# Splitting the state of a graph network's recurrence into two exact float32r parts for the aggregation by a 0/1 adjacency

## The chip, the cores and the metric

The kernel runs on one core of a Trainium2 chip. TensorE (PE in the profile) multiplies matrices and writes its results to PSUM; VectorE (DVE), ScalarE (ACT) and GpSimd (POOL) do elementwise work; SyncE (SP) issues the transfers. Each engine works through its own list of instructions in order, and waits at an instruction whose inputs are not there yet. The metric is the device time of one execution in microseconds (us), and the figure for a kernel is the median of its runs.

## The reference

The input is a batch of 128 graphs of 128 nodes with 256 features, and a 0/1 adjacency matrix for each graph. Four layers follow, each with a residual and a layer normalization:

- layer 0: attention with four edge types (scores by x scaled with a0 to a3, a softmax, a weighted sum of nodes),
- layer 1: a mean over neighbours of x W_msg, added to x W_upd, with a relu,
- layer 2: a gated recurrence of three steps,
- layer 3: attention by two vectors, a softmax, and an elu.

The change is in layer 2:

```
A = (adj != 0).astype(x.dtype)
h = x
for i in range(3):
    m = einsum('bnd,de->bne', h, weight[i])
    aggr = einsum('bst,bsd->btd', A, m)
    h = gru_cell(aggr, h, w_ih, w_hh, b_ih, b_hh)
```

All values are float32. The entries of A are 0 or 1.

## The kernel before

The 128 graphs are taken in 32 groups of four (G = 4, NG = 32), so that a tile of one half of the features (KC = 2 halves, c = 0 and 1, of 128) for a group is 128 x 512. A group passes through three generators: `head` (layers 0 and 1, ending with x2, the input of the recurrence), `gru` (layer 2, NL = 3 steps) and `tail` (layer 3 and the output).

The aggregation is moved ahead of the weight: since A^T (h W_i) w_ih^T = (A^T h) (W_i w_ih^T), the product W_i w_ih^T is made once at the start (c_gi, L158), and each step multiplies only the state h by the adjacency. `aggregate(c)` (L386 to L393) does that for one half of the features: four products of 128 x 128 by 128 x 128, one for each graph, with the state (nodes as rows, `hn[c]`) as the stationary operand and the mask a_ne as the moving one. ScalarE copies the result out of PSUM to agT (L393), which then multiplies c_gi in the gates (L401).

The state is kept with the features as rows (hT), as the gates want it. For the aggregation it must have the nodes as rows. In step 0, `hn` is a view of x2 itself (L367). In steps 1 and 2, `h_tokens` (L376) transposes hT by TensorE (L373) and copies the result out of PSUM: on ScalarE for c = 0, on VectorE for c = 1 (L378). For c = 0 it is called before the last gate of the step before (L467), for c = 1 after the first products of the step (L443), with two 128x512 products of L401 (L445, L446) between its transposes and `aggregate(1)`.

The gates follow: reset (L412), candidate (L418) and update (L426), each with ScalarE for the activation and VectorE for the arithmetic, and with one subtraction on GpSimd (L423).

While `gru` of group g runs, `head` of group g+1 and `tail` of group g-1 run beside it. `run` (L569) interleaves the three: each generator yields the TensorE time that it has just put out and the gap until it wants to go on, and `run` lets a side line go on when a clock made of these sums has passed its due time; a third value False says that the next piece has no TensorE work. This gives the order of TensorE's products. On the other engines the order in the built program is a list of its own, and pieces of different generators stand among each other there: on VectorE, the masks of the next group (L277) stand among the message step of this one (L343 to L351).

A layernorm (L183) goes over three engines: statistics on VectorE (L191, L192), a power on GpSimd (L196), then L198 and L201 on VectorE and L207 on ScalarE.

Tiles come from pools with a number of buffers for each tag: `hn` has 3, the layernorm's outputs have 2 (`xa`, x1 of layer 1), 4 (`xb`, shared by x2 and the output y) and 2 (`xa3`, x3 of layer 3). [...]

Of the kernel before, what the change touches and what calls it, by code (L numbers as in the profile page):

```python
# [7 lines left out]

F32 = mybir.dt.float32
U8 = mybir.dt.uint8  # L10
I32 = mybir.dt.int32
AF = mybir.ActivationFunctionType
# [5 lines left out]
def kernel(  # L18
# [30 lines left out]
    nc = tc.nc  # L49
    B, N, D = x.shape  # L50
    P = 128
    assert N == P and D == 2 * P
    G = 4
    NG = B // G
    T = G * N
    KC = D // P
# [49 lines left out]
    work = ctx.enter_context(tc.tile_pool(name="work", bufs=2))  # L106
# [76 lines left out]
    def layernorm(res, tag, bufs, out):  # L183


        mv = work.tile([P, G, 2], F32, tag="mv", name="mv", bufs=4)
        rstd = work.tile([P, G], F32, tag="rstd", name="rstd", bufs=4)
        nmr = work.tile([P, G], F32, tag="nmr", name="nmr", bufs=4)
        for b in range(G):
            st = work.tile([P, 6], F32, tag="st", name="st", bufs=8)  # L190
            nc.vector.bn_stats(st, res[:, b, :])  # L191
            nc.vector.bn_aggr(mv[:, b, :], st)  # L192
            if b == 1:
                yield 0.0, 1.5, False
        nc.vector.tensor_scalar_add(rstd, mv[:, :, 1], EPS)  # L195
        nc.gpsimd.tensor_tensor(rstd, rstd, neg_half, OP.pow)  # L196
        yield 0.0, 2.5, False
        nc.vector.scalar_tensor_tensor(nmr, mv[:, :, 0], -1.0, rstd, op0=OP.mult, op1=OP.mult)  # L198
        xn = work.tile([P, G, D], F32, tag=tag, name=tag, bufs=bufs)
        for b in range(0, G, 2):  # L200
            nc.vector.tensor_scalar(  # L201
                xn[:, b, :], res[:, b, :], mv[:, b, 0:1], rstd[:, b : b + 1],
                op0=OP.subtract, op1=OP.mult,
            )
        yield 0.0, 0.5, False
        for b in range(1, G, 2):
            nc.scalar.activation(  # L207
                xn[:, b, :], res[:, b, :], AF.Identity, bias=nmr[:, b : b + 1], scale=rstd[:, b : b + 1]
            )
        out.append(xn)  # L210
# [38 lines left out]
    def leaky(out, in_, bias):  # L249
        nc.scalar.activation(out, in_, AF.Prelu, bias=bias, scale=1.0, alpha=SLOPE)  # L250

    FLAT = "p b n -> p (b n)"


# [4 lines left out]
    def head(g, s):  # L259
# [8 lines left out]
        nc.gpsimd.memset(alpha, NEG0 / SLOPE)  # L268
        mk = work.tile([P, 4, G, N], U8, tag="mk", name="mk")
        s.m_gt = work.tile([P, G, N], U8, tag="m_gt", name="m_gt", bufs=3)  # L270
        s.a_ne = work.tile([P, G, N], F32, tag="a_ne", name="a_ne")


        xT = features_first(xg, "xT", 4)
# [1 line left out]
        for k in range(4):  # L276
            nc.vector.tensor_scalar(mk[:, k], a_f, float(k + 1), None, op0=OP.is_equal)  # L277
            yield 0.0, 1.0
            ps = bank()
            xs = []  # L280
            for c in range(KC):
                t = work.tile([P, T], F32, tag="xs", name="xs", bufs=4)
# [16 lines left out]
        got = []  # L299
# [6 lines left out]
        res = work.tile([P, G, D], F32, tag="res", name="res", bufs=3)  # L306
# [10 lines left out]
                )  # L317
        yield 1.75, 2.0, False
        got = []
        yield from layernorm(res, "xa", 2, got)  # L320
        x1 = got[0]
        yield 0.0, 2.0

# [30 lines left out]
            if b % 2:  # L354
                yield 0.9, 2.5, b == 1
        got = []
        yield from layernorm(res, "xb", 4, got)
        s.x2 = got[0]
        yield 0.0, 2.0
        s.hT = features_first(s.x2, "hT", 6)  # L360
        yield 0.9, 1.5

# [1 line left out]

    def gru(s):
        hT = s.hT
        hn = [s.x2[:, :, c * P : (c + 1) * P] for c in range(KC)]  # L367

        def tokens_first(c, h):

            ps = bank()
            for b in range(G):
                nc.tensor.transpose(ps[:, b * N : (b + 1) * N], h[:, b * N : (b + 1) * N], ident)  # L373
            return ps.rearrange("p (b d) -> p b d", b=G)

        def h_tokens(c, h):  # L376
            t = work.tile([P, G, P], F32, tag="hn", name="hn", bufs=3)
            (nc.scalar.copy if c == 0 else nc.vector.tensor_copy)(t, tokens_first(c, h))  # L378
            return t

        for i in range(NL):
            agT = [None] * KC
            new = [None] * KC
            gates = {}

            def aggregate(c):  # L386
                ps = bank()
                for b in range(G):
                    nc.tensor.matmul(  # L389
                        ps[:, b * N : (b + 1) * N], hn[c][:, b, :], s.a_ne[:, b, :], start=True, stop=True  # L390
                    )
                agT[c] = work.tile([P, T], F32, tag="agT", name="agT", bufs=3)
                nc.scalar.copy(agT[c], ps)  # L393

            def terms(q, of_h=(), of_m=(), start=False, stop=False):

                if start:
                    gates[q] = bank()
                ops = [(w_hhT[:, c], hT[c]) for c in of_h] + [(c_gi[:, i, c], agT[c]) for c in of_m]
                for n, (w, v) in enumerate(ops):  # L400
                    nc.tensor.matmul(  # L401
                        gates[q], w[:, q * P : (q + 1) * P], v,
                        start=(start and n == 0), stop=(stop and n == len(ops) - 1),
                    )
                return gates.pop(q) if stop else None

            def hidden(c, ps):
                t = work.tile([P, T], F32, tag="q", name="q", bufs=3)
                nc.scalar.activation(t, ps, AF.Identity, bias=bhn[:, c : c + 1], scale=0.5)  # L409
                return t  # L410

            def reset(c, ps, q):  # L412
                t = work.tile([P, T], F32, tag="t_r", name="t_r")
                nc.scalar.activation(t, ps, AF.Tanh, bias=brz[:, c : c + 1], scale=0.5)  # L414
                nc.vector.scalar_tensor_tensor(t, t, 1.0, q, op0=OP.add, op1=OP.mult)  # L415
                return t

            def candidate(c, ps, t):  # L418
                nc.vector.tensor_add(t, t, ps)  # L419
                n = work.tile([P, T], F32, tag="t_n", name="t_n")  # L420
                nc.scalar.activation(n, t, AF.Tanh, bias=bih[:, 2 * KC + c : 2 * KC + c + 1], scale=1.0)  # L421
                d = work.tile([P, T], F32, tag="t_d", name="t_d")
                nc.gpsimd.tensor_sub(d, hT[c], n)  # L423
                return n, d

            def update(c, ps, n, d):  # L426

                z = work.tile([P, T], F32, tag="t_z", name="t_z")
                nc.scalar.activation(z, ps, AF.Tanh, bias=brz[:, KC + c : KC + c + 1], scale=0.5)  # L429
                nc.vector.scalar_tensor_tensor(d, z, 1.0, d, op0=OP.add, op1=OP.mult)  # L430
                new[c] = work.tile([P, T], F32, tag="hT", name="hT", bufs=6)
                nc.vector.scalar_tensor_tensor(new[c], d, 0.5, n, op0=OP.mult, op1=OP.add)

            R, Z, C = 0, KC, 2 * KC
            aggregate(0)
            yield 0.9, 0.0
            terms(C, of_h=[0], start=True)
            terms(R, of_h=[0], start=True)
            yield 1.7, 0.0
            terms(C + 1, of_h=[0], start=True)  # L440
            yield 0.85, 0.0
            if i:
                hn[1] = h_tokens(1, hT[1])  # L443
                yield 0.45, 0.0
            q0 = hidden(0, terms(C, of_h=[1], stop=True))  # L445
            terms(R, of_h=[1])  # L446
            yield 1.7, 0.0
            aggregate(1)
            yield 0.9, 0.0
            q1 = hidden(1, terms(C + 1, of_h=[1], stop=True))  # L450
            yield 0.85, 0.0
            t0 = reset(0, terms(R, of_m=[0, 1], stop=True), q0)
            yield 1.7, 0.0
            n0, d0 = candidate(0, terms(C, of_m=[0, 1], start=True, stop=True), t0)
            yield 1.7, 0.0
            terms(Z, of_h=[0, 1], start=True)
            yield 1.7, 0.0
            update(0, terms(Z, of_m=[0, 1], stop=True), n0, d0)
            yield 1.7, 0.0
            terms(R + 1, of_h=[0, 1], start=True)  # L460
            yield 1.7, 0.0
            t1 = reset(1, terms(R + 1, of_m=[0, 1], stop=True), q1)
            yield 1.7, 0.0
            n1, d1 = candidate(1, terms(C + 1, of_m=[0, 1], start=True, stop=True), t1)
            yield 1.7, 0.0
            if i < NL - 1:
                first = h_tokens(0, new[0])  # L467
                yield 0.45, 0.0
            terms(Z + 1, of_h=[0, 1], start=True)
            yield 1.7, 0.0  # L470
            update(1, terms(Z + 1, of_m=[0, 1], stop=True), n1, d1)
            yield 1.7, 0.0
            if i < NL - 1:
                hn = [first, None]
            hT = new
        s.hT = hT
        s.tokens_first = tokens_first


    def tail(g, s):  # L480
# [4 lines left out]
            nc.vector.tensor_add(res[:, :, cols], s.tokens_first(c, s.hT[c]), s.x2[:, :, cols])  # L485
        yield 0.9, 2.0, False
        got = []
        yield from layernorm(res, "xa3", 2, got)
        x3 = got[0]
        yield 0.0, 2.0  # L490
        xT = features_first(x3, "xT", 4)
# [52 lines left out]
            nc.vector.scalar_tensor_tensor(res[:, half], neg[:, half], -1.0, res[:, half], op0=OP.add, op1=OP.add)  # L544
            yield 0.0, 1.0, False
        got = []
        yield from layernorm(res, "xb", 4, got)
        y = got[0]
        nc.sync.dma_start(out=out[g * G : (g + 1) * G].rearrange("b n d -> n b d"), in_=y)
        yield 0.0, 0.0  # L550
# [79 lines left out]
```

## Time and profile before

| | |
|---|---|
| median of 3 runs | 3250.92 us (3248.24 to 3251.22) |
| profiled execution | 3248.32 us, its span 3246.5 us |
| TensorE busy | 3172.2 us, 98% |
| VectorE, ScalarE, GpSimd busy | 1504.8, 1379.7, 724.7 us (46%, 42%, 22%) |
| granted TensorE clock | 0.993 |
| L401, gate products (two groups of 2304 records) | 1079.8 and 1072.7 us busy |
| L389, aggregation (1024 and 512 records) | 137.5 and 68.4 us busy |
| L373, transposes of the state (768 records) | 110.2 us busy |
| one group in the steady part (1029.65 to 1128.53 us) | 98.9 us |

The span is the time from the first to the last instruction of the profiled execution. A group's line in the profile names the source line, the engine, the operation, the tiles written and read, and the number of records; "mean ns" is the length of one record, which is longer than the distance between two of them, since TensorE's products overlap. The busy time counts overlapping records once. The idle time at the end of a line is that of the engine just before these instructions, with what ended it.

### The profile page before, as it was taken

The numbers are of one execution on the slowest core, as the hardware profiler recorded it, in microseconds if no ns is written. First come the engines' busy times: TensorE is split into PE (matmuls) and PEld (weight loads), VectorE is DVE, ScalarE is ACT, GpSimd is POOL, SyncE is SP. The second block draws the span as 40 slices with busy tenths as digits, with TensorE's granted clock in tenths as the row PEclk, the third lists the DMA queues.
The fourth block names the chain that finished last, engine by engine and source line by source line (L and its number), as shares of the span: only waits on it lengthen the run. The fifth ranks groups of instructions, "written<-read, shape, count | busy, mean of one in ns | idle before, by whom it ended". The sixth has DMA issues, their size and how long they took to land.

```text
span 3246.5 us, 33653 instructions
## 1 busy us (share of the span) xinstructions
PE 3172.2 (98%) x12244; PEld 1854.0 (57%) x12244; DVE 1504.8 (46%) x4019; ACT 1379.7 (42%) x2832; POOL 724.7 (22%) x615
## 2 busy tenths in 40 slices
PE   7999999999999999999999999999999999999996
PEld 5565555565555555555655555555556555555653
DVE  3454444544444544444444445444545344454443
ACT  3344444444444444444444444444444444444443
POOL 2122222222221222221222222222212222222211
PEclk9999999999999999999999999999999999999997
DMA  2000000000000000000000000000000000000000
GB/s 80 10 17 7 17 10 17 17 14 10 10 17 17 17 7 17 10 17 17 14 10 11 16 17 17 8 16 10 17 17 17 7 17 10 14 14 7 1 7 13
DMA packets 56997, 47.65 MB, mean 15 GB/s; under 512 B 4352, under 2 KB 56704, under 8 KB 56832
## 3 DMA queue, kind: packets, MB, share of 16 engines
q1 hardware_dynamic: 56832, 45.50, 4.4%
q8 instruction: 98, 1.61, 0.2%
q14 instruction: 67, 0.55, 0.1%
HBM read 28.72 MB, written 16.78 MB: 14 GB/s over the span
## 4 chain that ended last, share of the span: by engine, by line
PE 90%; DVE 5%; POOL 2%; ACT 1%; issue 1%; DMA 0%; SPq 0%; ACTq 0%; POOLq 0%; DVEq 0%
PE ps L401 56%; PE ps L291 7%; PE ps L332 7%; PE ps L389 5%; PE ps L219 4%; PE ps L497 4%; PE ps L373 2%; PE ps L530 2%; PE ps L341 2%; PE ps L311 2%; DVE mk L277 1%; POOL rstd L196 1%; POOL a_f L266 1%; PE ps L244 1%; DVE res L348 1%
## 5 line engine op out<-in xcount | busy, mean ns | idle before, releaser
L401 PE MATMUL ps<-agT,c_gi 128*128 128x512 f32 x2304 | 1072.7, 595 | 13.5 <-ACT agT L393 13.1
L401 PE MATMUL ps<-hT,w_hhT 128*128 128x512 f32 x2304 | 1079.8, 593 | 0.0
L401 PEld LDWEIGHTS ps<-agT,c_gi 128*128 128x128 f32 x2304 | 423.1, 190 | 512.5 <-issue 447.2
L401 PEld LDWEIGHTS ps<-hT,w_hhT 128*128 128x128 f32 x2304 | 410.6, 190 | 345.5 <-issue 325.0
L430 DVE SCALAR_TENSOR_TENSOR t_d<-t_z,t_d 128x512 f32<-128x512 f32 x192 | 132.4, 689 | 711.5 <-ACT t_z L429 711.5
L423 POOL TENSOR_TENSOR t_d<-hT,t_n 128x512 f32<-128x512 f32 x192 | 247.8, 1290 | 928.8 <-ACT t_n L421 928.8
L291 PEld LDWEIGHTS ps<-xs,xT 128*128 128x128 f32 x2048 | 248.7, 192 | 60.7 <-issue 46.6
L429 ACT ACTIVATE t_z<-ps,brz 128x512 f32<-128x512 f32 x192 | 131.9, 687 | 349.3 <-PE ps L401 349.3
L196 POOL TENSOR_TENSOR rstd<-rstd,neg_half 128x4 f32<-128x4 f32 x128 | 130.3, 1018 | 627.5 <-DVE rstd L195 627.3
L415 DVE SCALAR_TENSOR_TENSOR t_r<-t_r,q 128x512 f32<-128x512 f32 x192 | 132.4, 690 | 294.2 <-ACT t_r L414 294.2
L284 POOL TENSOR_SCALAR xs<-xT,acol 128x512 f32<-128x512 f32 x128 | 201.5, 1578 | 260.1 <-PE ps L291 166.5
L291 PE MATMUL ps<-xs,xT 128*128 128x128 f32 x2048 | 249.3, 275 | 0.0
L332 PE MATMUL ps<-w_um,xT 128*128 128x512 f32 x512 | 240.9, 594 | 0.5 <-ACT xT L220 0.5
L421 ACT ACTIVATE t_n<-t_r,bih 128x512 f32<-128x512 f32 x192 | 138.2, 720 | 212.7 <-DVE t_r L419 212.7
L409 ACT ACTIVATE q<-ps,bhn 128x512 f32<-128x512 f32 x192 | 131.1, 683 | 212.7 <-PE ps L401 212.7
L191 DVE BATCH_NORM_STATS2 st<-res 128x6 f32<-128x256 f32 x512 | 200.5, 408 | 2.1
L414 ACT ACTIVATE t_r<-ps,brz 128x512 f32<-128x512 f32 x192 | 130.8, 681 | 143.5 <-PE ps L401 139.5
L292 DVE COPY_PREDICATED alpha<-mk,ps 128x512 f32<-128x512 uint8 x128 | 93.1, 728 | 189.7 <-PE ps L291 189.7
L389 PEld LDWEIGHTS ps<-a_ne,hn 128*128 128x128 f32 x1024 | 132.7, 192 | 66.0 <-ACT q L409 31.7
L207 ACT ACTIVATE xb<-res,nmr,rstd 128x256 f32<-128x256 f32 x128 | 72.8, 595 | 218.0 <-DVE nmr L198 211.9
L332 PEld LDWEIGHTS ps<-w_um,xT 128*128 128x128 f32 x512 | 95.1, 191 | 108.3 <-issue 99.5
L419 DVE TENSOR_TENSOR t_r<-t_r,ps 128x512 f32<-128x512 f32 x192 | 131.8, 686 | 34.8 <-PE ps L401 28.2
(92 smaller groups left out, 3458.9 us busy)
## 6 DMA issues: line engine op xcount, KB each, us to landing
x_in<-in_x_dram SPq DMA_DIRECT2D x32, 512.0 KB, 3.9
out_dram<-xb SPq DMA_DIRECT2D x32, 512.0 KB, 2.9
adj_in<-in_adj_dram SPq DMA_DIRECT2D x32, 256.0 KB, 2.8
nat<-in_L_gnn_w_ih_dram SPq DMA_DIRECT2D x1, 768.0 KB, 4.9
wnat<-in_L_gnn_weight_dram SPq DMA_DIRECT2D x3, 256.0 KB, 5.2
nat<-in_L_gnn_w_hh_dram SPq DMA_DIRECT2D x1, 768.0 KB, 7.0
w_um<-in_L_gnn_W_upd_dram SPq DMA_DIRECT2D x1, 256.0 KB, 7.3
w_um<-in_L_gnn_W_msg_dram SPq DMA_DIRECT2D x1, 256.0 KB, 7.2
```

Source lines behind the costliest of these rows:

```text
L191: nc.vector.bn_stats(st, res[:, b, :])
L196: nc.gpsimd.tensor_tensor(rstd, rstd, neg_half, OP.pow)
L284: nc.gpsimd.tensor_scalar(t, xT[c], acol[:, k, c : c + 1], None, op0=OP.mult)
L291: nc.tensor.matmul(ps[:, cols], xT[c][:, cols], xs[c][:, cols], start=(c == 0), stop=(c == KC - 1))
L332: nc.tensor.matmul(ps, xT[c][:, b * N : (b + 1) * N], w_um[:, c, :], start=(c == 0), stop=(c == KC - 1))
L389: nc.tensor.matmul(ps[:, b * N : (b + 1) * N], hn[c][:, b, :], s.a_ne[:, b, :], start=True, stop=True)
L401: nc.tensor.matmul(gates[q], w[:, q * P : (q + 1) * P], v, start=(start and n == 0), stop=(stop and n == len(ops) - 1),)
L415: nc.vector.scalar_tensor_tensor(t, t, 1.0, q, op0=OP.add, op1=OP.mult)
L421: nc.scalar.activation(n, t, AF.Tanh, bias=bih[:, 2 * KC + c : 2 * KC + c + 1], scale=1.0)
L423: nc.gpsimd.tensor_sub(d, hT[c], n)
L429: nc.scalar.activation(z, ps, AF.Tanh, bias=brz[:, KC + c : KC + c + 1], scale=0.5)
L430: nc.vector.scalar_tensor_tensor(d, z, 1.0, d, op0=OP.add, op1=OP.mult)
```

## The change

The mask a_ne becomes a float32r tile. A new helper, `halves`, takes a piece of the state v and writes hi, v rounded to float32r, on ScalarE, and then lo = v - hi, also float32r, on an engine that is given. [...] `aggregate` multiplies hi and lo by the mask in turn and lets PSUM add them: eight products with float32r operands in place of four with float32.

In steps 1 and 2, `h_tokens` makes both parts from the transposed state in PSUM, hi on ScalarE and lo on VectorE, for both values of c. In step 0 the parts of x2 are made at the end of `head`, hi on ScalarE and lo on GpSimd, before x2's transposes, with yields of their own. `hi` and `lo` have 4 buffers each in place of the 3 of `hn`; the buffers of `xa`, `xb` and `xa3` go from 2, 4 and 2 to 1, 3 and 1.

```diff
@@ -7,6 +7,9 @@
 from concourse._compat import with_exitstack
 
 F32 = mybir.dt.float32
+
+
+F32R = mybir.dt.float32r
 U8 = mybir.dt.uint8
 I32 = mybir.dt.int32
 AF = mybir.ActivationFunctionType
@@ -249,6 +252,14 @@
     def leaky(out, in_, bias):
         nc.scalar.activation(out, in_, AF.Prelu, bias=bias, scale=1.0, alpha=SLOPE)
 
+    def halves(v, lo_engine):
+
+        hi = work.tile([P, G, P], F32R, tag="hi", name="hi", bufs=4)
+        lo = work.tile([P, G, P], F32R, tag="lo", name="lo", bufs=4)
+        nc.scalar.copy(hi, v)
+        lo_engine.tensor_sub(lo, v, hi.bitcast(F32))
+        return hi, lo
+
     FLAT = "p b n -> p (b n)"
 
 
@@ -268,7 +279,7 @@
         nc.gpsimd.memset(alpha, NEG0 / SLOPE)
         mk = work.tile([P, 4, G, N], U8, tag="mk", name="mk")
         s.m_gt = work.tile([P, G, N], U8, tag="m_gt", name="m_gt", bufs=3)
-        s.a_ne = work.tile([P, G, N], F32, tag="a_ne", name="a_ne")
+        s.a_ne = work.tile([P, G, N], F32R, tag="a_ne", name="a_ne")
 
 
         xT = features_first(xg, "xT", 4)
@@ -317,7 +328,7 @@
                 )
         yield 1.75, 2.0, False
         got = []
-        yield from layernorm(res, "xa", 2, got)
+        yield from layernorm(res, "xa", 1, got)
         x1 = got[0]
         yield 0.0, 2.0
 
@@ -354,9 +365,13 @@
             if b % 2:
                 yield 0.9, 2.5, b == 1
         got = []
-        yield from layernorm(res, "xb", 4, got)
+        yield from layernorm(res, "xb", 3, got)
         s.x2 = got[0]
-        yield 0.0, 2.0
+        yield 0.0, 1.0, False
+        s.hn = []
+        for c in range(KC):
+            s.hn.append(halves(s.x2[:, :, c * P : (c + 1) * P], nc.gpsimd))
+            yield 0.0, 0.5, c == KC - 1
         s.hT = features_first(s.x2, "hT", 6)
         yield 0.9, 1.5
 
@@ -364,7 +379,8 @@
 
     def gru(s):
         hT = s.hT
-        hn = [s.x2[:, :, c * P : (c + 1) * P] for c in range(KC)]
+
+        hn = s.hn
 
         def tokens_first(c, h):
 
@@ -374,9 +390,7 @@
             return ps.rearrange("p (b d) -> p b d", b=G)
 
         def h_tokens(c, h):
-            t = work.tile([P, G, P], F32, tag="hn", name="hn", bufs=3)
-            (nc.scalar.copy if c == 0 else nc.vector.tensor_copy)(t, tokens_first(c, h))
-            return t
+            return halves(tokens_first(c, h), nc.vector)
 
         for i in range(NL):
             agT = [None] * KC
@@ -386,9 +400,11 @@
             def aggregate(c):
                 ps = bank()
                 for b in range(G):
-                    nc.tensor.matmul(
-                        ps[:, b * N : (b + 1) * N], hn[c][:, b, :], s.a_ne[:, b, :], start=True, stop=True
-                    )
+                    for v in hn[c]:
+                        nc.tensor.matmul(
+                            ps[:, b * N : (b + 1) * N], v[:, b, :], s.a_ne[:, b, :],
+                            start=(v is hn[c][0]), stop=(v is hn[c][1]),
+                        )
                 agT[c] = work.tile([P, T], F32, tag="agT", name="agT", bufs=3)
                 nc.scalar.copy(agT[c], ps)
 
@@ -485,7 +501,7 @@
             nc.vector.tensor_add(res[:, :, cols], s.tokens_first(c, s.hT[c]), s.x2[:, :, cols])
         yield 0.9, 2.0, False
         got = []
-        yield from layernorm(res, "xa3", 2, got)
+        yield from layernorm(res, "xa3", 1, got)
         x3 = got[0]
         yield 0.0, 2.0
         xT = features_first(x3, "xT", 4)
@@ -544,7 +560,7 @@
             nc.vector.scalar_tensor_tensor(res[:, half], neg[:, half], -1.0, res[:, half], op0=OP.add, op1=OP.add)
             yield 0.0, 1.0, False
         got = []
-        yield from layernorm(res, "xb", 4, got)
+        yield from layernorm(res, "xb", 3, got)
         y = got[0]
         nc.sync.dma_start(out=out[g * G : (g + 1) * G].rearrange("b n d -> n b d"), in_=y)
         yield 0.0, 0.0
```

## The prediction

> **What bounds the kernel now.** I read the page first (busy shares and the chain that ended last), then the groups by form, then what TensorE waited for, then the timeline of one period. The page:
>
> ```profile
> PE 3172.2 (98%) x12244; PEld 1854.0 (57%) x12244; DVE 1504.8 (46%) x4019; ACT 1379.7 (42%) x2832; POOL 724.7 (22%) x615
> ...
> PE 90%; DVE 5%; POOL 2%; ACT 1%; issue 1%; DMA 0%; SPq 0%; ACTq 0%; POOLq 0%; DVEq 0%
> ```
>
> TensorE has work in 98% of the span and is 90% of the last chain; the other engines have room on average. So the time moves with TensorE's own work and with every new hole in it. The groups that the change touches, and two that serve as prices (the last number before the bar is the count, then busy us and mean ns of one):
>
> ```profile
> L423 POOL TENSOR_TENSOR t_d<-hT,t_n 128x512 f32<-128x512 f32 x192 | 247.8, 1290 | 928.8 <-ACT t_n L421 928.8
> ...
> L389 PE MATMUL ps<-a_ne,hn 128*128 128x128 f32 x1024 | 137.5, 277 | 9.3 <-DVE mv L192 9.3
> ...
> L419 DVE TENSOR_TENSOR t_r<-t_r,ps 128x512 f32<-128x512 f32 x192 | 131.8, 686 | 34.8 <-PE ps L401 28.2
> ...
> L389 PE MATMUL ps<-a_ne,xb 128*128 128x128 f32 x512 | 68.4, 277 | 0.0
> ...
> L378 DVE COPY hn<-ps 128x512 f32<-128x512 f32 x64 | 43.5, 679 | 3.4 <-PE ps L373 3.4
> ...
> L378 ACT COPY hn<-ps 128x512 f32<-128x512 f32 x64 | 37.2, 582 | 2.8 <-PE ps L373 1.0
> ```
>
> L389 is the aggregation: 32 groups x 3 layers x 2 halves x 4 graphs = 768 products, and 1536 records, so each float32 product is two passes. Its busy time is 205.9 us, 6% of the span: that is all the change can touch. What matters more is where TensorE waits inside a period (98.9 us, from one L373 of layer 2 at 1029.65 us to the same one at 1128.53). It waits at two places, once per period:
>
> ```profile
> PE ps L401 <- ACT agT L393: 13.1, 28, 0.5
> PE ps L389 <- DVE mv L192: 9.3, 28, 0.3
> ```
>
> Both belong to the second half (c = 1) of layer 2. The timeline there (start, duration, idle before in brackets), called place B:
>
> ```profile
> 1029.65 0.60 PE L373 MATMUL ps<-ident,hT 128*128 128x128 f32 x4
> ...
> 1031.47 0.68 DVE L378 COPY hn<-ps 128x512 f32<-128x512 f32 x1
> ...
> 1032.30 1.13 PE L389 MATMUL ps<-a_ne,hn 128*128 128x128 f32 x8 [0.33 <-DVE mv L192]
> ...
> 1033.25 1.01 POOL L196 TENSOR_TENSOR rstd<-rstd,neg_half 128x4 f32<-128x4 f32 x1 [2.13 <-DVE rstd L195]
> ...
> 1034.49 0.60 ACT L207 ACTIVATE xb<-res,nmr,rstd 128x256 f32<-128x256 f32 x1 [2.65 <-DVE nmr L198]
> 1034.99 0.56 ACT L393 COPY agT<-ps 128x512 f32<-128x512 f32 x1
> ...
> 1035.61 2.84 PE L401 MATMUL ps<-agT,c_gi 128*128 128x512 f32 x6 [0.47 <-ACT agT L393]
> ```
>
> The transposed state is ready at 1030.25, but the copy starts at 1031.47, behind the next graphs' message step on VectorE; the waiter's label (mv) is a neighbour, the copy is what ends at 1032.15. Then agT stands behind a layernorm line on ScalarE. The same step of layer 1, place A, lies 35 us earlier in a period:
>
> ```profile
> 994.46 0.60 PE L373 MATMUL ps<-ident,hT 128*128 128x128 f32 x4
> ...
> 995.33 0.67 DVE L378 COPY hn<-ps 128x512 f32<-128x512 f32 x1
> ...
> 996.31 0.16 DVE L195 TENSOR_SCALAR rstd<-mv 128x4 f32<-128x4 f32 x1
> 996.55 1.01 POOL L196 TENSOR_TENSOR rstd<-rstd,neg_half 128x4 f32<-128x4 f32 x1 [12.37 <-DVE rstd L195]
> 996.62 1.05 PE L389 MATMUL ps<-a_ne,hn 128*128 128x128 f32 x8
> ```
>
> Between the last transpose and the aggregation TensorE has two products of 0.86 us, so the copy has 1.72 us; here it finishes 0.6 us early.
>
> [...]
>
> **The change, part by part.**
> *TensorE.* Each product of two passes becomes two single-pass products (high, low), so 1536 passes stay 1536. Now eight passes of L389 take 0.89 us (1025.32 to 1026.21), 111 ns each. No row shows a float32r product. The nearest single pass over four-byte data is the transpose: L373, four from 1018.86 to 1019.30, 110 ns each, for 128 columns. [...] upper bound 222 ns (a whole float32 product each). I take 109: [...] Sum: 1536 x (109 - 111) = -3 us. Ends: [...] 1536 x +111 = +170 us.
>
> *Splitting the state, layers 1 and 2.* Before: one copy per half (ACT for c = 0, DVE for c = 1). After: ACT writes hi, then DVE subtracts: 64 more ACT copies at 582 ns (37 us) and 64 more DVE operations at 686 (44 us), against idle shares of 58% and 54%. For c = 0 this hides: after the transposes at 982.77 the aggregation comes at 990.55, 7.8 us for a chain of 0.6 + 0.7; in layer 2 (1018.86 to 1025.32) 6.5 us, and VectorE has idle time before L343 that takes the subtraction up but for 0.1 us. Were that cover gone, 0.7 us each.
>
> For c = 1 it does not hide. Without any queue the chain is 0.60 (transposes) + 0.58 + 0.69 + hand-overs of some 0.1 = 2.0 us against 2.16; all queueing comes on top, and the built order of the changed kernel shows what stands ahead.
>
> Place A: ScalarE has hi behind two of the exp lines (L232); VectorE has lo behind the whole layernorm of the head: all four L191, L516, L227, then L195, L198 (which waits for the power on GpSimd) and both L201. From 992.60, at the spacings of before (L191 0.32, L516 0.60, L227 0.59, with L192 0.08 to 0.1): L516 starts at 994.14 instead of 993.34, the maximum L227 ends at 995.58, L195 at 995.66, the power runs to 996.75, L198, two L201, lo from 997.53 to 998.20. hi is there at 997.0 (two exp at 0.40 from 995.61, then 0.58). The first low product starts at 998.27, seven more passes, and the next product at 999.04 instead of 997.51: 1.53 us late. agT, which costs a gap of 0.28 in the products behind it now (the row of four at 998.37 takes 2.17 instead of 1.88), is then in time. Net 1.25 us.
>
> Place B: VectorE has one mask (L277), one L191 and one L192 more ahead of lo than it had ahead of the copy (0.33 + 0.33 + 0.08), so lo runs 1032.26 to 1032.94 and the aggregation ends 0.5 us later. The layernorm behind it slides too: L195 1033.06, power to 1034.32, L207 at 1034.55 and 1035.05. ScalarE's order is now both L207, hi of the next group's x2 (0.6, itself waiting for the second L207), and only then agT: 1036.2 to 1036.8. TensorE's L401 resumes at 1036.85 instead of 1035.61: 1.24 us. The first half's delay lies inside this.
>
> Sum: 2.5 us per period. 28 periods show both old waits; I count 29 for edges: 72 us.
>
> *x2's own halves, layer 0.* Two ACT copies and two POOL subtractions (1290 ns by L423) a group: on POOL from 1036.3 to 38.9, before L423 needs it at 1041.3; TensorE needs them a good 10 us later. The one uncovered case is the first group, where aggregation follows at once: some 2 us, once.
>
> *Order and buffers.* TensorE's order is unchanged but for the x2 transposes, one pair of products later, with 6.9 us until use: nothing. xa and xa3 at one buffer: x1 lives until L351 and x3 until L540, within one period each: nothing. xb at three: y takes the buffer of the x2 that its tail read first, x2 that of a y sent out almost a period before: nothing; a wait would cost about a power round trip, 1.3 us a period. The mask a_ne in float32r: same count and shape, nothing. DMA is untouched.
>
> Total: -3 + 72 + 2 = +71 us on the profiled 3248.3 (span 3246.5), 3319. The median of the runs stands 2.6 higher, 3250.9, so 3322; I say 3321.
>
> **Rivals.**
> (1) A float32r product of only 128 columns costs as much as a float32 product. For: nothing shows that the single pass is quick at this shape. Against: the transposes. +170 in place of -3, of which place B's sixth (28) hides behind agT's wait: 3321 + 173 - 28 = 3466.
> (2) The one that ends faster: [...] Outside place B 1280 passes gain 111 - p. It decides at p = 111 - 74/1.28 = 53 ns with waits as worked, at p = 111 - 38/1.28 = 81 with waits half as long (36 us, and the 2 of the start). [...]
> (3) The waits do not come, since the layernorm ahead of lo runs earlier than I put it: 3321 - 72 = 3249, no change.
>
> **How the numbers follow.** Forecast 63%, own range 3285 to 3360 (1.2 to 3.8 us a period). (1) 17%. (2) 14%: half of it faster, the rest split between equal and slower. (3) 6%. The range 3225 to 3400 leaves out (1) and the lower end of (2), two in ten. Faster or slower means by more than 0.2%, 6.5 us, about what a measurement of this kernel can tell from no change: faster 0.07, same 0.08, slower 0.85.
>
> **What would show it.** Aggregation passes 109 to 112 ns apart: the even trade; [...] TensorE's waits: the subtraction ahead of the aggregation some 1.3 us, once a period, place A; agT ahead of L401 grown from 0.47 to above 1 us, place B. A period of 101.4 us instead of 98.9. I am wrong if the period is within 0.3 us of the old one, or if waits appear at c = 0 or layer 0.

## The result and the profile after

The changed kernel takes 3358.61 us (median of 4 runs, 3358.08 to 3360.88) against 3250.79 us for the kernel before in the same measurement: a ratio of 1.0335, 95% interval 1.0317 to 1.0353. Its profiled span is 3356.9 us, 110.4 us more than the 3246.5 of before. That hi is the state rounded to float32r, and that hi and lo together give it back exactly, as the title has it, is the intent of the change; no run here measures it.

The page of the changed kernel, busy time and the chain that ended last:

```profile
PE 3196.9 (95%) x12244; PEld 1864.5 (56%) x12244; DVE 1563.8 (47%) x4083; ACT 1457.8 (43%) x2960; POOL 794.2 (24%) x679
...
PE 62%; DVE 22%; ACT 7%; POOL 5%; issue 3%; DMA 0%; ACTq 0%; DVEq 0%; POOLq 0%; SPq 0%
```

TensorE has exactly the 12244 records of before, and its share of the last chain has gone from 90% to 62%, with VectorE from 5% to 22%. TensorE's waits (who waited for whom, us in total, times, longest):

```profile
PE ps L404 <- DVE lo L260: 71.5, 61, 2.3
PE ps L417 <- ACT agT L409: 30.0, 28, 1.1
```

These stand where before had 9.3 and 13.1 us. (L404 is the aggregation, L417 the gate products, L260 the subtraction, L409 the copy to agT.) Place A, the second half of the state in layer 1, on all engines:

```profile
1027.03 1.11 POOL L199 TENSOR_TENSOR rstd<-rstd,neg_half 128x4 f32<-128x4 f32 x1 [11.52 <-DVE rstd L198]
...
1027.69 0.56 ACT L259 CAST hi<-ps 128x512 fp32r<-128x512 f32 x1
...
1028.17 0.16 DVE L201 SCALAR_TENSOR_TENSOR nmr<-mv,rstd 128x4 f32<-128x4 f32 x1 [0.90 <-POOL rstd L199]
1028.25 0.73 DVE L204 TENSOR_SCALAR xa<-res,mv,rstd 128x256 f32<-128x256 f32 x2
...
1028.31 0.33 PE L404 MATMUL ps<-a_ne,hi 128*128 128x128 f32 x1 [0.24 <-ACT hi L259]
...
1028.90 0.68 DVE L260 TENSOR_TENSOR lo<-ps,hi 128x512 fp32r<-128x512 f32 x1
...
1029.63 0.33 PE L404 MATMUL ps<-a_ne,lo 128*128 128x128 f32 x1 [1.00 <-DVE lo L260]
...
1030.47 1.72 PE L417 MATMUL ps<-hT,w_hhT 128*128 128x512 f32 x2
...
1031.98 4.69 PE L417 MATMUL ps<-agT,c_gi 128*128 128x512 f32 x8
...
1133.97 1.07 PE L417 MATMUL ps<-hT,w_hhT 128*128 128x512 f32 x2
...
1134.88 3.60 PE L417 MATMUL ps<-agT,c_gi 128*128 128x512 f32 x8
```

The high part is ready at 1028.25. VectorE, though, is in the layernorm: it waits 0.90 us for GpSimd's power, then writes xa twice, and only then subtracts. TensorE stands still for most of that time: it waits 0.24 us for hi, runs one product, and waits 1.00 us for lo. The last four lines are the next thing that TensorE does, in this period and in the next one. The same ten passes take 6.04 us from 1030.47 to the next product, and 4.34 us one period later. No wait lies in them: the granted clock is 0.59 in the 4 us from 1030.00 (0.50 from 1030.76 to 1034.17) and 1.00 in the 4 us from 1133.00. The stretches of the changed kernel (from:to, length, then busy time of each engine, and the granted TensorE clock ahead of the DMA share):

```profile
1030.00:1034.00 4.00, 4.00 (x11) 2.03 (x11) 0.00 (x0) 1.86 (x4) 0.19 (x1) 0.59 0.00 0
...
1133.00:1137.00 4.00, 3.87 (x14) 2.22 (x15) 0.26 (x2) 2.56 (x7) 0.53 (x1) 1.00 0.00 0
```

Place B, the second half in layer 2:

```profile
1067.77 0.33 PE L404 MATMUL ps<-a_ne,lo 128*128 128x128 f32 x1 [1.31 <-DVE lo L260]
...
1069.32 1.09 ACT L210 ACTIVATE xb<-res,nmr,rstd 128x256 f32<-128x256 f32 x2 [3.06 <-DVE nmr L201]
1070.45 0.62 ACT L259 CAST hi<-xb 128x512 fp32r<-128x512 f32 x1
1070.97 0.58 ACT L409 COPY agT<-ps 128x512 f32<-128x512 f32 x1
...
1071.60 2.84 PE L417 MATMUL ps<-agT,c_gi 128*128 128x512 f32 x6 [1.07 <-ACT agT L409]
```

Here ScalarE has agT behind both of its writes of xb and behind the first copy of x2. Before, agT stood between the two writes of xb, and there was no copy of x2.

TensorE's starts give an account of a steady period, 98.88 us before and 101.80 after, and 103.50 in ten of the 30 periods, with one exception every third. From the transposes of place A to the probabilities' transposes (L244 before, L247 after) it is 7.62 us before and 9.06 after: +1.44. From the transposes of place B to the second product on agT it is 5.96 and 7.53: +1.57. The other steps differ by little, -0.1 in all. The periods of 103.50 have 1.70 more, half of the 3.41 us for which the granted clock is 0.50. Over the 30 periods the sum is 103 us, of which some 86 are waits and some 17 (ten periods) the clock. The other 7 lie at the start and the end.

### The profile page after: what moved, and what is told of

Read it like the earlier page. It is cut to its first block, busy times and chain, and to the rows that moved or that the text cites. A ratio compares the mean times of both kernels' runs of the same rounds, so it can differ in the third digit from the quotient of the medians.

```text
span 3356.9 us, 33791 instructions
## 1 busy us (share of the span) xinstructions
PE 3196.9 (95%) x12244; PEld 1864.5 (56%) x12244; DVE 1563.8 (47%) x4083; ACT 1457.8 (43%) x2960; POOL 794.2 (24%) x679
## 3 DMA queue, kind: packets, MB, share of 16 engines
q8 instruction: 97, 1.59, 0.2%
## 4 chain that ended last, share of the span: by engine, by line
PE 62%; DVE 22%; ACT 7%; POOL 5%; issue 3%; DMA 0%; ACTq 0%; DVEq 0%; POOLq 0%; SPq 0%
PE ps L417 43%; PE ps L302 7%; PE ps L513 3%; PE ps L222 3%; DVE st L194 3%; POOL rstd L199 3%; PE ps L404 3%; POOL res L556 2%; DVE hT L448 2%; ACT xb L210 2%; DVE lo L260 2%; DVE res L325 1%; DVE res L359 1%; PE ps L389 1%; DVE t_d L446 1%
## 5 line engine op out<-in xcount | busy, mean ns | idle before, releaser
L417 PE MATMUL ps<-agT,c_gi 128*128 128x512 f32 x2304 | 1076.2, 599 | 30.0 <-ACT agT L409 30.0
L417 PE MATMUL ps<-hT,w_hhT 128*128 128x512 f32 x2304 | 1089.4, 597 | 0.0
L417 PEld LDWEIGHTS ps<-agT,c_gi 128*128 128x128 f32 x2304 | 429.5, 193 | 515.7 <-issue 459.3
L417 PEld LDWEIGHTS ps<-hT,w_hhT 128*128 128x128 f32 x2304 | 413.3, 191 | 359.7 <-issue 339.7
L404 PE MATMUL ps<-a_ne,lo 128*128 128x128 f32 x768 | 185.5, 280 | 72.1 <-DVE lo L260 71.5
L404 PE MATMUL ps<-a_ne,hi 128*128 128x128 f32 x768 | 225.5, 328 | 7.1 <-ACT hi L259 7.1
L404 PEld LDWEIGHTS ps<-a_ne,lo 128*128 128x128 f32 x768 | 147.4, 192 | 106.9 <-DVE lo L260 90.4
L404 PEld LDWEIGHTS ps<-a_ne,hi 128*128 128x128 f32 x768 | 147.4, 192 | 55.5 <-ACT hi L259 32.0
```

The lines of the kernel that those rows point to most:

```text
L404: nc.tensor.matmul(ps[:, b * N : (b + 1) * N], v[:, b, :], s.a_ne[:, b, :], start=(v is hn[c][0]), stop=(v is hn[c][1]),)
L417: nc.tensor.matmul(gates[q], w[:, q * P : (q + 1) * P], v, start=(start and n == 0), stop=(stop and n == len(ops) - 1),)
```

## The experiments

I began with the theory of the prediction: passes trade evenly, and the chain of high and low part is too long for its cover at A and B. Its main rival was that the float32r products cost. Neither survived as it stood; a third theory came from the first four runs.

**The products alone.** One float32r copy for each half, on the engines of before, multiplied twice.

```diff
-                for b in range(G):
-                    for v in hn[c]:
-                        nc.tensor.matmul(..., v[:, b, :], s.a_ne[:, b, :],
-                            start=(v is hn[c][0]), stop=(v is hn[c][1]))
+                for b in range(G):
+                    for n in range(2):
+                        nc.tensor.matmul(..., hn[c][:, b, :], s.a_ne[:, b, :],
+                            start=(n == 0), stop=(n == 1))
```

> The products alone. The state is copied once into one float32r tile, on the engines of before (ACT for c = 0, DVE for c = 1; ACT for x2), and that tile is multiplied twice in place of hi and lo; there is no subtraction, and the low part is left out. Theory (the passes trade evenly at 111 ns, the whole loss is waits behind the subtraction): 1536 passes as before, waits of before, 3245 to 3275 us. Rival (the float32r products themselves cost more, or upset the products around them): most of the 108 us remain, 3320 or more.

It took 3318.65 us, a ratio of 1.0210 (1.0194 to 1.0225). That is above the range of the theory, and just under the 3320 of the rival: some 68 us of the loss are there with no subtraction in the kernel. TensorE's waits in it:

```profile
PE ps L396 <- DVE hn L384: 47.0, 60, 1.2
PE ps L409 <- ACT agT L401: 45.8, 30, 1.6
```

**The split alone.** The same hi and lo as in the change, one float32 product of lo.

```diff
-        lo = work.tile([P, G, P], F32R, tag="lo", name="lo", bufs=4)
+        lo = work.tile([P, G, P], F32, tag="lo", name="lo", bufs=4)
...
-                    for v in hn[c]:
-                        nc.tensor.matmul(..., v[:, b, :], s.a_ne[:, b, :], ...)
+                    nc.tensor.matmul(..., hn[c][1][:, b, :], s.a_ne[:, b, :], start=True, stop=True)
```

> The split alone. hi and lo are made as in the change, in the same places and on the same engines, but lo and the mask are float32 and the aggregation is one float32 product of lo, two passes as before; the high part is left out of the result. Theory (waits behind the subtraction): as slow as the change, 3340 to 3370 us, with the subtraction ahead of the aggregation and agT ahead of the gates in TensorE's waits. Rival (the products): close to before, 3250 to 3270.

It took 3251.22 us, 1.0001 (0.9992 to 1.0009): no loss at all, with every ScalarE copy and every VectorE and GpSimd subtraction of the change in it. Its waits are those of before:

```profile
PE ps L415 <- ACT agT L407: 14.9, 28, 0.5
...
PE ps L403 <- DVE lo L260: 7.8, 30, 0.5
```

So the chain of two operations fits where the list is this one, and the theory fell. What tells the change and the products alone from the kernel before and the split alone is the order of the lists in the built programs. VectorE at place A, around the score selection (alpha), by the tile written (COPY and LO are the second half's copy and subtraction):

```
before     alpha mv st nmax mv st COPY mv m_gt rstd nmr xa xa
split      alpha mv st nmax mv st m_gt mv rstd LO nmr xa xa
products   st mv st mv alpha mv nmax rstd m_gt nmr xa COPY xa
change     st mv st mv alpha mv nmax rstd m_gt nmr xa xa LO
```

nmr waits for GpSimd's power. In the first two lists the copy or the subtraction stands ahead of it, in the last two behind. ScalarE at place B, in the same way (X2 is a copy of x2):

```
before     xb agT q xb
split      xb agT q xb X2 X2
products   xb xb X2 agT X2
change     xb xb X2 agT X2
```

The lists go with the number of product instructions that the source puts out for an aggregation: four in the first two, eight in the others. By what rule the builder orders them is not shown.

**One float32r product.** As the products alone, with the second product taken out (`for n in range(2)` gone).

> As the products alone, but with one float32r product in place of two: 768 passes fewer, the low part left out. Theory: a pass costs 111 ns of TensorE's time in its place, so 768 x 0.111 = 85 us below the products alone, 3165 to 3190 us. [...] rival (twice a pass): 170 below.

It took 3213.35 us, 0.9885 (0.9868 to 0.9901). That is 105 us below the products alone, and above the range expected, which had put the products alone near the kernel before. Its list on VectorE has the copy where before has it, and its list on ScalarE has agT between the two xb: with four products in place of eight, and float32r as in the products alone, the order of before is back. TensorE's order is the same in before, in this kernel and in the products alone; this one and the products alone differ only by the 768 products and by what the builder made of them. TensorE's busy time fell by 85.2 us between the two (3173.7 to 3088.5), which is 111 ns a pass. Against the kernel before only 37 us of this reach the end: the waits for agT grew from 13.1 to 55.7 us.

**The buffers alone.** The kernel before with `xa` and `xa3` at 1 and `xb` at 3.

> The kernel before with the change's numbers of buffers for the layernorm's outputs alone (xa and xa3 at 1, xb at 3). Theory: no instruction waits for a buffer, 3251 us within 7. Rival (part of the loss is waits for a buffer): 3265 or more.

3250.26 us, 1.0000 (0.9991 to 1.0008), as expected.

**High products first.** The loops over the parts and over the graphs changed places.

```diff
-                for b in range(G):
-                    for v in hn[c]:
+                for v in hn[c]:
+                    for b in range(G):
```

(`start` and `stop` are then set once for the bank.)

> The change with the four high products of an aggregation ahead of its four low ones, in place of high and low in turn for each graph. Theory (TensorE stands before the first low product, and the hole lets the clock fall): three more passes of 0.11 us run inside each hole, so 0.33 us less at places A and B, 0.67 us a period, 20 us over 30 periods, and some or all of the clock's falls (nine times 1.7 us) go with the shorter holes: 3320 to 3345 us. Rival (the wait is not before the first low product): 3359 as the change.

3329.62 us, 1.0242 (1.0227 to 1.0257), 29 us less than the change. Place A is 0.33 us shorter, as worked out, and the clock no longer falls in the steady part (granted 0.993 over the run, as before; 0.988 in the change). At place B the 0.33 is lost again to the wait for agT (39.3 us in all).

**The hole filled.** Eight products more on TensorE ahead of the second aggregation.

```diff
+                if i and c == 1:
+                    for n in range(8):
+                        nc.tensor.matmul(ps[:, :N], hn[c][0][:, 0, :], s.a_ne[:, 0, :], start=True, stop=True)
```

> The change with TensorE kept busy in the holes: in steps 1 and 2, for c = 1, eight more products of the high part of the first graph stand ahead of the aggregation, overwritten by it, so the result is the same. Eight passes are 0.89 us, and TensorE waits some 1.2 us there for the low part. Theory (the clock is granted at half for one window of 3.4 us every third period [...]): the waits keep their length, the falls of the clock in the steady part go, and 10 to 20 us with them: 3340 to 3350 us. Rival (the falls have another cause): they stay, 3359 us or more.

The clock did not fall once in the steady part (granted 0.994 over the run), as the theory said, and every period is 102.32 us. But the time is 3359.87, no gain, and above the range expected: against the change's own 101.80 us for a period without a fall, 0.5 us came in. The builder put the second of the two copies of x2 ahead of agT too on ScalarE, and the wait for agT at place B grew from 1.07 to 1.59 us a period. So with TensorE kept busy at place A the falls of the clock did not come; the fill does not show why, nor what a fall costs; the cost is read from the periods of 101.80 and 103.50 us.

**More cover, after and before.** The update gate's two products on the hidden state go ahead of `aggregate(1)`.

```diff
+            terms(Z, of_h=[0, 1], start=True)
+            yield 1.7, 0.0
             aggregate(1)
...
-            terms(Z, of_h=[0, 1], start=True)
-            yield 1.7, 0.0
             update(0, terms(Z, of_m=[0, 1], stop=True), n0, d0)
```

In the change:

> The change with the two products of the update gate's hidden part (Z, c = 0) moved ahead of the second half's aggregation, so that four products of 0.43 us x 2 passes stand between the transposes and the aggregation instead of two: 1.72 us more cover. Theory (the chain of hi and lo is 1.2 to 1.7 us late and nothing else is): the waits for lo go at A and mostly at B, agT may still stand behind the layernorm on ScalarE; 3240 to 3290 us. Rival (the engines that split are short of throughput, so a wait comes back further on): 3320 or more.

3254.37 us, 1.0011 (1.0002 to 1.0019). VectorE's lists at places A and B are the change's, with the layernorm first at A, and the wait for lo is all but gone; agT's is not:

```profile
PE ps L417 <- ACT agT L409: 41.2, 30, 1.4
...
PE ps L404 <- DVE lo L260: 1.1, 2, 0.6
```

Place B in this run:

```profile
1040.45 1.14 ACT L259 CAST hi<-xb 128x512 fp32r<-128x512 f32 x2
1041.49 0.58 ACT L409 COPY agT<-ps 128x512 f32<-128x512 f32 x1
...
1042.12 4.56 PE L417 MATMUL ps<-agT,c_gi 128*128 128x512 f32 x10 [1.40 <-ACT agT L409]
```

The rival fell: the engines are not short of throughput, and 1.72 us of other products hide what the place in VectorE's list cost. They do not hide the place in ScalarE's list at place B, since agT comes after the aggregation: both writes of xb and now both copies of x2 stand ahead of it. In the kernel before:

> The same move of the two products in the kernel before. Theory: the two waits of before, 0.33 and 0.47 us a period, and the 0.28 at place A shrink or go, 28 x 0.8 to 1.1 = 22 to 31 us at most: 3220 to 3245 us. Rival (the move lets the planner's order of the other lines fall worse, or a PSUM bank is held too long): 3251 or more.

3205.85 us, 0.9859 (0.9843 to 0.9876): faster than both kernels with all arithmetic in float32. A period is 97.37 us, 1.5 shorter, more than the 0.8 to 1.1 of visible waits that I had put up as the most, and the time is below the range expected. No wait for agT is left in this kernel. So under the same cover the change is still 48.5 us slower than the kernel before, 1.58 us a period, of which 1.40 are the wait for agT at place B.

**VectorE's order alone, both ways.** In the change, the subtraction pinned ahead of rstd and of the masks; in the kernel before, the copy pinned behind both writes of xa at place A, with TensorE's order held as it was.

```diff
+        with tc.issue_after(latest[0]):          # the change: rstd and the masks after lo
             nc.vector.tensor_scalar_add(rstd, mv[:, :, 1], EPS)
...
+            tc.add_manual_dep(latest[0], done.ins.name, ...)   # before: the copy after the last xa
```

> The change with VectorE's order alone altered: for c = 1 the subtraction is pinned ahead of the layernorm's step before the power (rstd) at place A, and ahead of that and of the masks at place B; TensorE's order is the change's own. Theory of the order (what the doubled products cost is the place of the second half's copy or subtraction on VectorE): the wait for lo shrinks at both places; agT then stands behind the layernorm that slid back, so 0.8 to 1 us a period comes back and the clock's falls go, 3300 to 3335 us. Rival (the chain of hi and lo itself is what is too long): 3350 to 3360 us.

3320.68 us, 1.0215 (1.0200 to 1.0230), 38 us back out of 108. The wait for lo fell from 71.5 to 25.8 us, the clock's falls went (granted 0.993 over the run), and agT's wait rose from 30.0 to 49.8. ScalarE's list was not pinned: at place B both copies of x2 stand ahead of agT (a wait of 1.48 us a period), and at place A agT is behind a layernorm that is now later (0.18).

> The kernel before, with float32 products, one copy and no split, and TensorE's order as it is, but with the copy of the second half pinned behind both L201 of the layernorm at place A, where the change has its subtraction. Theory of the order: the copy ends 1.9 us later there, 0.28 of agT's gap comes back, 1.6 us a period, 28 to 30 periods: 3290 to 3305 us, with neither float32r nor a subtraction in it. Rival (the order is harmless, the float32r products or the split make it slow): 3251 us within 7.

3360.85 us, 1.0341 (1.0324 to 1.0358): a loss as large as the change's, in a kernel with float32 products and no split, by the place of one copy a period. Its waits:

```profile
PE ps L400 <- DVE hn L387: 70.8, 31, 5.5
PE ps L413 <- ACT agT L405: 13.1, 28, 0.5
PE ps L400 <- DVE mv L194: 9.2, 28, 0.3
```

I had 1.6 us a period, and the time is above the range expected. A period without a fall of the clock is 101.0, 2.1 longer than before; most are 102.7, with a fall. The size is the change's, the make-up is not: place B is as before, place A loses more than in the change, because the statistics ahead of it keep the order of before and the layernorm ends later, and the clock falls 23 times in place of ten, some 39 us (granted 0.981 over the run, 0.988 in the change). The run shows that the place of one copy can cost this much, and not that each part of the change's loss is this one.

**Where a float32r pass does pay.** The gate products, 512 columns, with hT and w_hhT as float32r tiles.

```diff
-    w_hhT = const.tile([P, KC, 3 * D], F32, name="w_hhT")
+    w_hhT = const.tile([P, KC, 3 * D], F32R, name="w_hhT")
...
-                new[c] = work.tile([P, T], F32, tag="hT", name="hT", bufs=6)
+                new[c] = work.tile([P, T], F32R, tag="hT", name="hT", bufs=6)
```

> A measurement of a float32r product of 512 columns: in the kernel before, the state hT and the weights w_hhT are float32r tiles, so the gate products of the hidden state (1152 of 128x512) are single passes of rounded operands; the aggregation is float32 as before. Part of the precision is left out. Theory 1 [...]: 0.43 us a product instead of 0.86, 1152 x 0.43 = 495 us less if nothing else binds, 2755 us. Theory 2 [...] The distance between two such products in the trace tells them apart.

2738.44 us in a single timed execution. Five such products in a row on TensorE:

```profile
1059.03 1.42 PE L402 MATMUL ps<-hT,w_hhT 128*128 128x512 f32 x5
```

The five start 0.32, 0.23, 0.24 and 0.23 us apart: after a longer first step, some 0.235 us a product of 512 columns, against two passes of 0.43 in float32 (in the kernel before, four passes of L401 from 994.90 to 996.62, 1.72 us). The 1152 products are 1152 records, where before had 2304. So the 0.43 us of Theory 1 did not come, although the time lies next to its 2755: TensorE now waits for other engines, 103.4 us at the transposes of the state (L374) alone, and the granted clock is 0.966 in place of 0.993.

> The kernel before with all gate products of the recurrence in float32r (hT, agT, w_hhT and c_gi rounded, one pass each), and the update gate's two products moved ahead of the second aggregation as in the cover runs; part of the precision is left out. A pass of 512 columns at 0.235 us in place of two at 0.43 takes 2304 x 0.62 = 1430 us of TensorE's work away; VectorE, busy 1526 us, and the chains between the engines then set the time. Theory: faster than the hidden-state gates alone (2738 us), 2200 to 2600 us, with TensorE under 85% busy. Rival (the chain is already bound by the other engines at 2738): 2700 or more.

2278.73 us, 0.7010 (0.7000 to 0.7021), with TensorE busy 84%. It is faster than both kernels by far, but it gives the state, agT and the gate weights to the gates as float32r, where the kernel before and the change give them as float32; what this does to the result is not measured here, and whether it may be is for the user of the network to say.

## Why the prediction was right, and where it was not

*Sign and range.* Slower was forecast, 3321 with a range of its own of 3285 to 3360; 3358.6 lies at the top of it. The forecast put the change 71 us above before; it measured 108 by the medians, 110 in the profiled execution. Some 86 us of this are waits, where 72 were forecast; with these alone the time would have been some 3337. That 3358.6 is still inside the range is due to the width of the range, since no term of the sum foresaw the clock.

*TensorE's passes.* Right: aggregation passes stand 112 ns apart (median), as before, and 768 passes taken out gave 85.2 us, 111 ns each. I had 109, which no trace of before shows; they show 110 for the transposes and 111 for the aggregation, and with 111 the sum moves by 3 us. A float32r product of 512 columns takes 0.235 us, so 128 columns would take some 59 ns by that rate (an estimate); the number of columns alone does not account for the 111. What does is not shown. By the same token the transposes, my nearest row, were no evidence on the time of a longer product.

*The halves c = 1, places A and B.* The mechanism that I traced is the one in the trace: lo behind the power and two writes of xa at A, agT behind the layernorm and x2's copy at B. The sizes were 1.25 and 1.24 us, measured 1.44 and 1.57. What failed is the step's heading: I booked the 72 us to the split ("For c = 1 it does not hide"). The split alone costs nothing (1.0001) where the lists are favourable; the products alone cost 68 us, and one float32 copy in the wrong place of VectorE's list costs as much as the change (3360.85 us against 3358.61), with the falls of the clock that it brings. The term belongs to the builder's order on VectorE and ScalarE, which moved with the count of products. What the copies of x2 on ScalarE add at place B, once they stand ahead of agT, was not measured apart. I had read that order, and put it down as the queue behind which the chain happened to stand.

*What was left out.* The clock. A stall was priced by its own length; ten times it also cost 1.70 us of half clock after it, 17 us in all. The rest of the gap is the start and the end, 7 us where I had 2.

*c = 0, layer 0, buffers, GpSimd.* Right for the waits named: the time between TensorE's starts around c = 0 and layer 0 agrees with before within 0.2 us, and the buffers cost nothing. Only x2's copies on ScalarE were not free where they stood ahead of agT.

*The rivals.* (1) and (2) fell with the 111 ns. (3), that the waits would not come, is what the split alone showed for a better list; in the change they came.

## What to carry to other kernels

An edit that only multiplies instruction counts on one engine can reshuffle what the builder lists on another: compare the lists around every short hand-over, and price what stands ahead there as the edit's cost. Put cover between a transpose and the product that needs its copy (here 1.72 us of products that could go earlier), and the place of that copy in its list stops costing (here the wait for lo went from 71.5 to 1.1 us). Then look at the next hand-over: the cover did nothing for agT, which is made after the aggregation (a wait of 41.2 us, 30.0 without the cover). What float32r gained went with the shape: nothing at 128 columns, where it had to run twice (112 ns a pass, as before), while the gate products of 512 columns went from 0.86 to some 0.235 us, a bit over a quarter.

## What the runs showed of the hardware

In the steady part of the change the granted TensorE clock fell to 0.50 for single stretches of 3.41 us. One of them, with the columns as above (it is 1.00 in the 3.41 us before and after):

```profile
1030.76:1034.17 3.41, 3.41 (x5) 1.35 (x4) 0.00 (x0) 1.18 (x2) 0.00 (x0) 0.50 0.00 0
```

A fall costs 1.70 us (a period of 103.50 in place of 101.80). The falls of the steady part come after the hole at place A. TensorE's stillness there, as the time from the transposes to the product after the aggregation less the 3.05 us of before: 1.07 us (order pinned), 1.34 (high first) and 1.46 (products alone) gave no fall in the steady part; 1.67 (the change) gave ten, and 2.7 (copy late) gave 23.

The length of a wait alone does not decide. At place B of the products alone TensorE waits longer at a stretch than at place A of the change (0.24 and 1.00 us), in 28 periods, and the clock never fell in the steady part (granted 0.993 over the run):

```profile
1059.36 2.84 PE L409 MATMUL ps<-agT,c_gi 128*128 128x512 f32 x6 [1.56 <-ACT agT L401]
```

The ten stretches of the change start 307.2 us apart, three periods, and once 204.8, two periods. What makes the clock fall is not shown.

Writing float32r took no longer than writing float32: ScalarE's copy out of PSUM 578 ns (582 before), the subtraction 687 ns on VectorE and 1277 on GpSimd (686 and 1290 for the float32 operations of L419 and L423 in the kernel before).
